# Cross attention with layer norm: 128 instead of 64 rows of weights in each score matmul

## The chip, the core and the metric

The kernel runs on one core of a Trainium2 chip. The time is device microseconds for one execution, and the median over runs is given. The core has a matrix engine (TensorE, PE in the profile; PEld are its weight loads), a vector engine (DVE), a scalar engine (ACT), GpSimd (POOL), a queue engine (SP), and DMA engines that move data beside them. Matmuls write to PSUM, which has eight banks.

## The reference

Four batches, 2048 queries of 512 features each, 77 context rows per batch, 16 heads of 32 features. A mask excludes context rows; the output is normalised over the features with a gain and an offset.

```python
qs = (q @ wq).reshape(Bq, Lq, H, HD).transpose(0, 2, 1, 3)
ks_ = (k @ wk).reshape(Bq, Lk, H, HD).transpose(0, 2, 1, 3)
vs = (v @ wv).reshape(Bq, Lk, H, HD).transpose(0, 2, 1, 3)
scores = jnp.einsum('bhqd,bhkd->bhqk', qs, ks_) / jnp.sqrt(jnp.float32(HD))
scores = jnp.where(mask[:, None, :, :], -jnp.inf, scores)
attn_w = jax.nn.softmax(scores, axis=-1)
attn = jnp.einsum('bhqk,bhkd->bhqd', attn_w, vs)
attn = attn.transpose(0, 2, 1, 3).reshape(Bq, Lq, H * HD)
out = attn @ wo + q
mu = jnp.mean(out, axis=-1, keepdims=True)
var = jnp.mean((out - mu) ** 2, axis=-1, keepdims=True)
return (out - mu) / jnp.sqrt(var + EPS) * gamma + beta
```

## The kernel before

The 8192 rows of x are cut into 64 tiles of 128 rows; a pair of tiles is a block, and four tiles are a group. The order of all work is written out by hand in the string `ORDER`, one letter per step and a number for the tile, block or group; each engine works through its own share of that order, first in, first out for DVE, ACT, POOL and the SP queue. Buffers and PSUM banks are assigned by hand in `SLOTS`.

For each group the steps are: load x transposed (`g`, L260 to L262, on SP), split it into a high and a low part (`i` on ACT, L265; `j` on POOL, L269), project to queries with three products of the parts (`Q`, L275, 12 matmuls of 128x128 weights and 512 streamed columns for each of four column blocks), and copy the queries out of PSUM (`q`, L289, DVE).

For each tile t: the scores (`S`, L391 to L408, PE), the masked maxima out of PSUM (`T`, L416, DVE, 16 heads one by one), the exponentials with their sums (`e`, L431, ACT), reciprocals (`r`, L441, DVE), normalisation (`n`, L446, POOL), and a transposition in blocks of 32 (`t`, L467, DVE). For each block: regrouping of the transposed weights by twelve DMAs (`P`, L478, mostly on SP), the product with the values (`V`, L492, PE, weights of 96x32), copies of its high and low part (`a`, L521, ACT; `b`, L525, DVE). For each tile again: the output projection (`O`, L548, PE, 12 matmuls), the residual (`+`, L557, DVE), the moments (`s`, L568, L569, DVE), the scale (`v`, `k`, POOL and ACT), gain and offset (`f`, L587, L588, POOL), and the store (`w`, L591, SP). The last 16 tiles take a shorter way at the end (L594 to L617), with the residual added by matmuls with an identity (`X`, L537) for the last eight.

The scores of a tile: heads lie four to a 128-partition column block of the queries, 32 partitions each. For head group g (four of them) and head j within it (four), the weights are the queries of that head, 32 partitions by `SR` rows, and the streamed side is the 77 keys. Each j writes to a PSUM bank of its own (four banks a tile), each g to its own 77 columns of it, and each slice of `SR` rows to its own partitions. With `SR = 64` a weight tile has 32 rows and 64 columns of the array, and eight such tiles fit into the array; the inner loops run over the two row slices and then the four heads. Both operands are 32-bit floats, and a matmul of these leaves two weight loads and two multiplies in the trace.

```python
for g in range(NG):
    for r0 in range(0, P, SR):
        for j in range(GH):
            q = slice(HD * j, HD * (j + 1))
            mm = nc.tensor.matmul(
                sc[j][r0 : r0 + SR, g * NK : (g + 1) * NK],
                qs[q, g, rs.start + r0 : rs.start + r0 + SR],
                kct[q, g, t // TPB, keys_of(j)],
```

In the steady middle the order on PE for a block is: scores of one tile, product with the values of an earlier block, scores of the other tile, two query projections (24 matmuls), two output projections (24 matmuls).

Of the kernel before, what the change touches and what calls it, by code (L numbers as in the profile page):

```python
# [37 lines left out]
MASKED = -3.38e38  # L38
EPS = 1.0e-5
WARM = 9  # L40
SR = 64
NPB = 3
KSCALE = 1.0 / HD**0.5
LATE = 48
# [129 lines left out]
def xattn_layernorm(  # L174
# [75 lines left out]
    def keys_of(h):  # L250
        return slice(TAIL_K, NK2) if h % 2 == 0 else slice(0, NK)
# [139 lines left out]
    def scores(t):  # L391
# [3 lines left out]
# [8 lines that stand above are left out]
# [357 lines left out]
```

## Time and profile before

| what | value |
|---|---|
| median of 3 runs | 526.71 us (525.96 to 527.35) |
| span of the profiled execution | 525.7 us |
| instructions in the profile | 20274 |
| score loads and multiplies (L399) | 4096 and 4096 |
| granted TensorE clock | 0.997 |

The profiled execution's own time is known by its span, from its first to its last instruction; the 1.0 us between it and the median lies around the span. PE's busy time adds up records whose ends are modelled and which overlap, so a group's busy time is its union in time, and the mean of one record is longer than its share. A timeline row gives the start, the length of the merged stretch, engine, line, operation and count, and in brackets the idle time before it and what ended it.

### The profile page before, as it was taken

How to read it: one execution, taken by the hardware profiler on the slowest of the kernel's cores; microseconds unless marked ns; L12 is line 12 of the kernel's file. 1: busy time of each engine (PE TensorE's matmuls, PEld its weight loads, DVE VectorE, ACT ScalarE, POOL GpSimd, SP SyncE). 2: the span in 40 equal slices, each digit the busy share in tenths (PEclk: the TensorE clock that was granted, in tenths of full speed). 3: DMA queues.
4: the chain of work that ended last, by engine and by line, in shares of the span. 5: the costliest groups of instructions: out<-in, count | busy, mean ns of one | idle time of the engine just before them, and what ended most of it. 6: DMA issues, size and time to landing. Idle time of an engine off the chain costs nothing.

```text
span 525.7 us, 20274 instructions
## 1 busy us (share of the span) xinstructions
PE 507.2 (96%) x6845; PEld 388.8 (74%) x6845; DVE 476.0 (91%) x2572; ACT 460.4 (88%) x2215; POOL 405.5 (77%) x371
## 2 busy tenths in 40 slices
PE   9999999999989999999999999999999999999994
PEld 6987777778767777777777777767777777767662
DVE  5798988989979989998989989998998999999997
ACT  6699999998989999999999999999999999987400
POOL 2475736889889889969989887988888689869551
PEclk9999999999999999999999999999999999999998
DMA  8948577785797677988887687797868987388555
GB/s 300 401 125 241 148 205 196 195 236 147 205 243 226 189 197 225 217 219 219 215 225 207 178 224 226 184 254 195 213 190 225 259 251 189 91 219 218 158 176 199
DMA packets 59261, 110.85 MB, mean 211 GB/s; under 512 B 9430, under 2 KB 11758, under 8 KB 59158
## 3 DMA queue, kind: packets, MB, share of 16 engines
q1 hardware_dynamic: 55702, 102.75, 69.1%
q0 software_dynamic: 2496, 5.77, 3.9%
q10 hardware_dynamic: 960, 1.05, 0.8%
q8 instruction: 54, 0.88, 0.7%
q14 instruction: 49, 0.40, 0.3%
HBM read 41.79 MB, written 16.78 MB: 111 GB/s over the span
## 4 chain that ended last, share of the span: by engine, by line
PE 51%; DVE 12%; DMA 10%; POOL 9%; SPq 9%; ACT 5%; issue 3%; POOLq 0%; DVEq 0%
PE pq L275 20%; PE po L548 15%; PE sc L399 7%; SPq L478 6%; PE pa L492 6%; DMA PT<-B 6%; ACT pbuf L431 4%; POOL o L587 3%; DVE B L467 3%; POOL o L588 2%; POOL pbuf L446 2%; DVE pbuf L416 2%; PE pv L326 2%; DMA stage_a<-xT 1%; POOL xtl L269 1%
## 5 line engine op out<-in xcount | busy, mean ns | idle before, releaser
L431 ACT ACTIVATE pbuf<-pbuf,nm 128x77 f32<-128x77 f32 x1024 | 352.7, 350 | 16.2 <-DVE nm L416 13.4
L431 ACT ACTIVATION_READ_ACCUMULATOR pbuf<-pbuf,nm 128x1 f32 x1024 | 194.6, 190 | 0.0
L416 DVE CUSTOM_DVE_ANT_0 pbuf<-sc,mb 128x77 f32<-128x77 f32 x1024 | 170.2, 231 | 9.6 <-PE sc L399 8.5
L446 POOL TENSOR_TENSOR pbuf<-pbuf,ri 128x1232 f32<-128x1232 f32 x63 | 142.8, 2267 | 39.4 <-DVE ri L441 23.6
L467 DVE STREAM_TRANSPOSE B<-pbuf 128x1280 f32<-128x1280 f32 x64 | 96.1, 1502 | 9.8 <-POOL pbuf L446 5.4
L548 PE MATMUL po<-woh,AH 128*128 128x512 f32 x256 | 102.6, 401 | 0.0
L548 PE MATMUL po<-woh,AL 128*128 128x512 f32 x256 | 100.1, 391 | 2.3 <-DVE AL L525 2.3
L275 PE MATMUL pq<-xth,wqh 128*128 128x512 f32 (+1 forms) x256 | 101.8, 398 | 0.2
L548 PE MATMUL po<-wol,AH 128*128 128x512 f32 x256 | 99.8, 390 | 0.0
L275 PE MATMUL pq<-xtl,wqh 128*128 128x512 f32 (+1 forms) x256 | 98.3, 384 | 0.0
L275 PE MATMUL pq<-xth,wql 128*128 128x512 f32 (+1 forms) x256 | 98.1, 383 | 0.0
L416 DVE DVE_READ_ACCUMULATOR2_ANT nm<- 128x1 f32 x1024 | 83.9, 82 | 0.0
L399 PEld LDWEIGHTS sc<-kct,q 32*64 32x64 f32 x4096 | 52.8, 130 | 32.9 <-issue 17.1
L587 POOL TENSOR_TENSOR o<-o,gam 128x512 f32<-128x512 f32 x48 | 62.5, 1302 | 13.7 <-ACT o L583 13.4
L269 POOL TENSOR_TENSOR xtl<-xtf,xth 128x1024 fp32r<-128x1024 f32 x28 | 67.3, 2403 | 6.7 <-ACT xth L265 6.6
L399 PE MATMUL sc<-kct,q 32*64 32x77 f32 x4096 | 63.6, 238 | 8.4 <-issue 3.8
L588 POOL TENSOR_TENSOR o<-o,bet 128x512 f32<-128x512 f32 x48 | 62.4, 1300 | 3.8
L492 PE MATMUL pa<-PT,vsb 96*32 96x256 f32 x992 | 59.9, 382 | 0.0
L521 ACT CAST AH<-pa 128x512 fp32r<-128x512 f32 x64 | 36.4, 572 | 25.0 <-DVE st L596 10.6
L548 PEld LDWEIGHTS po<-woh,AL 128*128 128x128 f32 x256 | 48.0, 188 | 13.8 <-DVE AL L525 3.5
L548 PEld LDWEIGHTS po<-woh,AH 128*128 128x128 f32 x256 | 48.0, 188 | 13.7 <-issue 2.0
L275 PEld LDWEIGHTS pq<-xth,wqh 128*128 128x128 f32 x256 | 48.1, 188 | 12.0 <-PE sc L399 0.5
(108 smaller groups left out, 666.0 us busy)
## 6 DMA issues: line engine op xcount, KB each, us to landing
PT<-B SPq DMA_DIRECT2D x343, 128.0 KB
xtf<-xT SPq DMA_DIRECT2D x28, 512.0 KB
o<-x SPq DMA_DIRECT2D x56, 256.0 KB
out<-o SPq DMA_DIRECT2D x56, 256.0 KB
PT<-B POOLq DMA_DIRECT2D x25, 128.0 KB, 3.8
xtf<-xT SPq DMA_DIRECT2D x4, 256.0 KB
stage_a<-wq SPq DMA_DIRECT2D x4, 256.0 KB
stage_a<-wk SPq DMA_DIRECT2D x4, 256.0 KB
```

The source lines that it names most:

```text
L269: nc.gpsimd.tensor_tensor(l[:, c : c + 2], fx.pop((g, c)), xh[g][:, c : c + 2].bitcast(F32), ALU.subtract)
L275: nc.tensor.matmul(pq, w[:, c, m * P : (m + 1) * P], r[g][:, c, rs], start=(n == 0), stop=(n == 11))
L399: mm = nc.tensor.matmul(sc[j][r0 : r0 + SR, g * NK : (g + 1) * NK], qs[q, g, rs.start + r0 : rs.start + r0 + SR], kct[q, g, t // TPB, keys ...
L416: nc.vector.tensor_tensor_reduce(pb[:, h // 2, (h % 2) * NK : (h % 2 + 1) * NK], scs[t][j][:, g * NK : (g + 1) * NK], mb[:, t % TPB, keys_ ...
L431: nc.scalar.activation(pb[:, h // 2, (h % 2) * NK : (h % 2 + 1) * NK], pb[:, h // 2, (h % 2) * NK : (h % 2 + 1) * NK], AF.Exp, bias=nmax[t ...
L446: nc.gpsimd.tensor_tensor(pv, pv, rv.to_broadcast((P, NP, 2, NK)), ALU.mult)
L467: nc.vector.transpose(bt.rearrange("p c q r -> p q c r"), pbuf[t % NPB].rearrange("p q (c r) -> p q c r", c=5),)
L492: nc.tensor.matmul(pas[b, g // 2][HD * j : HD * (j + 1), (g % 2) * BLK : (g % 2 + 1) * BLK], vsb[:, 2 * b // TPB, h % 2, HD * (h // 2) : H ...
L521: nc.scalar.copy(*at_part(once(ahs, b, [P, NG, BLK], F32R, "AH"), b, i, by_tile))
L548: nc.tensor.matmul(pos[t], a[:, c, rs], w[:, c, :], start=(first and c == 0 and n == 0), stop=(c == NC_D - 1 and n == 2),)
L587: nc.gpsimd.tensor_tensor(o, o, gam, ALU.mult)
L588: nc.gpsimd.tensor_tensor(o, o, bet, ALU.add)
```

## The change

One constant is doubled. The loop over row slices in `scores` then has one pass, and every score matmul takes the 128 rows of a tile as weights.

```diff
 EPS = 1.0e-5
 WARM = 9
-SR = 64
+SR = 128
 NPB = 3
 KSCALE = 1.0 / HD**0.5
```

A tile then has 16 score matmuls in the program in place of 32. Each has weights of 32 partitions by 128 columns, streams the same 77 keys, and writes all 128 partitions of its bank's 77 columns. Such a weight tile takes 32 rows and 128 columns of the array, and four of them fit. No other function reads the constant.

## The prediction

> **What bounds the kernel now.** I read the page first, then the busy time by stretches, then one period of the middle as a timeline, then the score matmuls alone.
>
> ```profile
> span 525.7 us, 20274 instructions
> ...
> PE 507.2 (96%) x6845; PEld 388.8 (74%) x6845; DVE 476.0 (91%) x2572; ACT 460.4 (88%) x2215; POOL 405.5 (77%) x371
> ```
>
> ```profile
> 22.00:132.05 110.05, 109.14 (x1556) 85.12 (x1557) 100.77 (x607) 105.22 (x527) 77.94 (x55) 1.00 0.69 194
> 132.05:283.63 151.58, 148.35 (x2081) 114.81 (x2081) 138.94 (x786) 145.07 (x697) 132.18 (x112) 1.00 0.79 213
> 283.63:298.38 14.75, 14.75 (x209) 11.45 (x209) 14.01 (x80) 13.74 (x65) 12.90 (x12) 1.00 0.77 217
> 283.63:406.06 122.43, 119.00 (x1666) 91.99 (x1665) 111.06 (x630) 114.75 (x552) 106.74 (x89) 1.00 0.78 212
> 406.06:479.80 73.74, 72.80 (x1143) 53.63 (x1143) 70.22 (x420) 71.34 (x370) 58.88 (x58) 1.00 0.75 208
> 479.80:525.70 45.90, 37.33 (x280) 25.69 (x276) 42.18 (x101) 11.66 (x48) 22.93 (x41) 0.97 0.58 181
> ```
>
> The columns are the stretch and its length, then the busy time of PE, weight loads, DVE, ACT and POOL, the granted clock, the DMA share and GB/s. From 22 to 480 us, where all score matmuls lie, PE is busy for 449.3 of 457.8 us at the full clock, and in the period 283.63 to 298.38 (two tiles of 128 rows) for all of it. DVE is next with 14.01 of 14.75. After 479.8 DVE leads, but no score matmul runs there. So a microsecond added to PE before 480 is a microsecond on the end, less what PE's few waits swallow:
>
> ```profile
> PE sc L399 <- issue: 3.8, 4, 1.6
> PE po L548 <- DVE AL L525: 2.3, 3, 1.0
> PE sc L399 <- DMA o<-x: 2.0, 2, 1.3
> ...
> PE sc L399 <- DVE q L289: 0.9, 2, 0.7
> PE sc L399 <- DMA PT<-B: 0.6, 1, 0.6
> PE sc L399 <- DVE nm L416: 0.6, 2, 0.4
> ```
>
> These are all of PE's waits at the score matmuls but one of 0.2 us, in total, times and longest: 3.8 + 2.0 + 0.9 + 0.6 + 0.6 = 7.9 us. The 2.3 us of L548 belong to the tail.
>
> Now one period on PE:
>
> ```profile
> 283.63 0.95 PE L399 MATMUL sc<-kct,q 32*64 32x77 f32 x64
> ...
> 284.51 1.93 PE L492 MATMUL pa<-PT,vsb 96*32 96x256 f32 x32
> ...
> 286.38 0.95 PE L399 MATMUL sc<-kct,q 32*64 32x77 f32 x64
> ```
>
> One tile's scores are 64 pairs of a weight load and a multiply (the program has 32 matmuls a tile, and each leaves two pairs in the trace). From their first start to the start of what comes next is 284.51 - 283.63 = **0.88 us**. What sets these 0.88 us is seen by counting how many have started by a given time:
>
> ```profile
> 283.62:283.69 0.07, 0.06 (x8) 0.06 (x9) 1.00 1.12 234
> ...
> 283.62:283.75 0.13, 0.12 (x9) 0.12 (x17) 1.00 0.83 205
> 283.62:283.81 0.19, 0.18 (x16) 0.18 (x24) 1.00 0.83 237
> 283.62:283.88 0.26, 0.25 (x24) 0.25 (x32) 1.00 0.94 268
> 283.62:283.94 0.32, 0.31 (x32) 0.31 (x33) 1.00 0.95 250
> 283.62:284.05 0.43, 0.42 (x37) 0.42 (x37) 1.00 0.83 233
> 283.62:284.15 0.53, 0.52 (x44) 0.52 (x49) 1.00 0.80 236
> ...
> 283.62:284.35 0.73, 0.72 (x63) 0.72 (x64) 1.00 0.85 275
> ```
>
> The counts in brackets are multiplies and loads. The first 32 multiplies come in rounds of eight, one for each of the eight 32x64 tiles: 8, 16, 24, 32, the last three counts 0.065 us apart, and the loads run one round ahead. The second round starts (9th multiply) just before 283.75, about 0.117 after the first. So in this half the multiplies' streaming decides, about 0.067 us a round, and the loads are hidden. The other 31 need 0.41 us, and now loads and multiplies start together (37 and 37): nothing lies ready, so this half is paced by the issue of instructions, about 13 ns a pair. The last multiply has started just after 284.35, and the next work starts some 0.15 us later.
>
> **The change part by part.** It halves the pairs of a tile (64 to 32, so 4096 to 2048 in the run), and makes each one wider: 128 columns of weights go into a 32x128 tile, of which there are four. The streamed side stays at 77 columns. The four tiles do the work of eight in the same eight rounds (32 / 4 = 64 / 8). By streaming alone nothing changes, and the issue gets twice the room. What grows is the weight load.
>
> ```profile
> L399 PEld LDWEIGHTS sc<-kct,q 32*64 32x64 f32 x4096 | 52.8, 130 | 32.9 <-issue 17.1 <-DVE nm L416 8.8 <-DMA PT<-B 3.9
> L275 PEld LDWEIGHTS pq<-xtl,wqh 128*128 128x128 f32 x256 | 48.2, 188 | 8.9 <-POOL xtl L269 0.3 <-issue 0.2
> ```
>
> ```profile
> 23.87 0.19 PEld L275 LDWEIGHTS pq<-xth,wqh 128*128 128x128 f32 x1 [0.26 <-PE sc L399]
> 23.98 0.19 PEld L275 LDWEIGHTS pq<-xtl,wqh 128*128 128x128 f32 x1
> 24.10 0.19 PEld L275 LDWEIGHTS pq<-xth,wql 128*128 128x128 f32 x1
> 24.23 0.19 PEld L275 LDWEIGHTS pq<-xth,wqh 128*128 128x128 f32 x1
> 24.34 0.19 PEld L275 LDWEIGHTS pq<-xtl,wqh 128*128 128x128 f32 x1
> ```
>
> A load of 64 columns lasts 130 ns in the records and one of 128 columns 188: 58 ns for 64 columns. With the array idle, a second load of 128 columns starts 0.11 us after the first (23.87, 23.98). So I price a load at about 0.053 us for 64 columns and 0.107 for 128, behind a fixed latency that is hidden. The counts fit: the second round begins a load and a stream (0.053 + 0.064) after the first, later ones a stream.
>
> The Trainium skill (TensorE: Matmul & The Clock Gate, section "LDWEIGHTS (loading the stationary operand)") says that a 32x128 load takes as long as a 128x128 one, since the columns count and not the rows. No run here shows a 32x128 load; by that rule the sum below would stand as it is.
>
> Today's 0.053 hides under the 0.067 of a round. The new 0.107 doesn't: a tile of the array takes its next weights once the multiply before has begun (the loads are one round ahead, never two), so its period is the load, and the 0.067 of streaming lies under it. I take 0.110 a round (0.11 between the two loads). Low end: 0.107, nothing between loads. High end: 0.120, the spacing of the loads at 24.10, 24.23, 24.34, each beside a multiply.
>
> A tile's scores then: first load 0.107, seven rounds of 0.110 = 0.770, the four tiles' starts 7 ns apart (eight starts in the first 0.06 us) 0.02, and 0.155 from the last start to the next work: 1.052 us in place of 0.88, **+0.17 us**, times 64 tiles **+10.9 us**. With 0.107 it is +0.149 and +9.5; with 0.120 +0.24 and +15.4.
>
> Given back: PE's issue stalls.
>
> ```profile
> q8 instruction: 54, 0.88, 0.7%
> ```
>
> ```profile
> 252.92 0.95 PE L399 MATMUL sc<-kct,q 32*64 32x77 f32 x64
> 253.81 1.93 PE L492 MATMUL pa<-PT,vsb 96*32 96x256 f32 x32
> 255.67 0.80 PE L399 MATMUL sc<-kct,q 32*64 32x77 f32 x46
> 257.38 0.42 PE L399 MATMUL sc<-kct,q 32*64 32x77 f32 x18 [0.90 <-issue]
> ```
>
> Fetched instructions came in 54 packets, 16 KB each. The 6845 pairs are 13,690 instructions, so these look like PE's own, some 250 a packet. In the stall at 257.38 the scores stand still inside a tile, with no engine behind it: since 252.92 PE had used up 128 + 64 + 92 instructions. After the change this whole stretch has 64 + 64 + 64, less than a packet, so such stalls should mostly go: of 3.8 us I take 2.2 back (bounds 0 and 3.8). Of the 4.1 us of waits for DMA and DVE, a slower PE swallows some, since whoever is late gains 0.34 us a period: 1.5 (bounds 0 and 4.1). DVE's maxima (L416) start 0.17 us later in each tile, covered by PE's own lateness: ACT, POOL and the DMAs behind them have the same work in a longer period. Banks, semaphores and the order of the program stay; no DMA is added, none moved.
>
> Sum: 525.7 + 10.9 - 2.2 - 1.5 = 532.9 us of span. The median of the runs is 526.71, 1.0 above this execution's span, so **533.9 us**, 1.4% slower. Own range: 526.7 + 9.5 - 7.9 = 528.3 to 526.7 + 15.4 = 542.1.
>
> **The rivals.**
>
> *Faster: wide loads are as quick as two narrow ones.* Today the two 64-column tiles over the same 32 rows must both be filled within a round, 2 x 0.053 in 0.067, so they load side by side. If one 128-column load uses both ways, it takes 0.053 and hides, and eight rounds of streaming remain, all out of the queue: 0.053 + 7 x 0.067 + 0.02 + 0.155 = 0.70, -0.18 a tile, -11.7 in all, with 2.2 of stalls -13.9. DVE's 14.01 in a period of 14.75 leaves room, but waits for DVE and DMA would grow; I count two thirds, -9.3: 517.4. Against it: 128-column loads follow each other at 0.11 even where nothing else runs. It decides as soon as a load stays under 0.067. Chance 0.13.
>
> *No change: the first load is hidden.* If the first wide load of a tile is put under the tail of the work before, a tile costs 0.945, +0.065, times 64 +4.2, less 3.7: 527.2. Against it: loads of the scores stand 0.35 us idle before each tile.
>
> ```profile
> 283.63 0.79 PEld L399 LDWEIGHTS sc<-kct,q 32*64 32x64 f32 x64 [0.35 <-issue]
> ```
>
> Chance 0.08.
>
> *Far slower: a load waits for its own tile's multiply.* The period is then 0.107 + 0.067 = 0.174, a tile 0.107 + 7 x 0.174 + 0.175 = 1.50, +0.62, times 64 +39.7; with all 6.3 us of DMA and DVE waits and fetch stalls swallowed (2.2 + 4.1) it ends at 560. Against it: rounds of 0.067 with loads of 0.053 in them, and projections that follow each other at 0.12 with a load of 0.107 beside each. That the four tiles run one after another, so that the change doesn't do what it says, would be 32 x 0.107 + 0.175 = 3.6 us a tile, +2.7, times 64 +174: 700; today's eight run at once, and I count it in here. Chance of both 0.05.
>
> The Trainium skill (TensorE: Matmul & The Clock Gate, section "The mechanism" of the packing part) states this rule: a load overlaps running matmuls only where the row group differs. Here each row group always has its own multiply running, so by it the result would be this rival's 560; the rows just named speak against it.
>
> **How the numbers follow.** Forecast 0.74, rivals 0.13, 0.08 and 0.05. A difference of 0.3% (1.6 us) is about what these runs can tell from none. Faster takes the first rival and a little of the second, 0.14; same takes most of the second and the forecast's lowest corner, 0.10; slower is 0.76. The range runs from 526 to 543: it holds the forecast's own and the second rival, and leaves out 0.18.
>
> **What would show it.** The scores' multiplies should be 2048, 32 a tile, in rounds of four about 0.11 us apart, with a load at the start of each round and its multiply after it; first start to next start about 1.05 us; loads of about 188 ns; a period near 15.1 us with PE full; fewer "issue" stalls inside tiles. Rounds at 0.067 show the first rival, at 0.17 the third. If tiles take 1.05 us and the end still doesn't move, the step from PE's time to the end was wrong; if the issue stalls stay, that of the fetch.

## The result and the profile after

| | kernel before | kernel after |
|---|---|---|
| median, 20 runs each | 526.48 us (523.44 to 531.38) | 529.10 us (527.63 to 531.17) |
| ratio | 1 | 1.0042, 95% interval 1.0023 to 1.0061 |
| profiled execution: span | 525.7 us | 526.0 us |

The kernel became 2.6 us slower where 7.2 us were forecast: sign and range held, the size did not. The profiled execution of the new kernel took 527.80 us for its span of 526.0, so 1.8 us lie around the span, and not the 1.0 that the prediction had from the median. The profiled execution of before, with the same 1.8, was one of about 527.5, 1.1 above its median; the one of after lies 1.3 below its own. That is why the spans differ by 0.3 us and the medians by 2.6.

The page of the kernel after, its head, the fetch queue and the chain of waits:

```profile
span 526.0 us, 16084 instructions
...
PE 514.5 (98%) x4797; PEld 398.4 (76%) x4797; DVE 477.8 (91%) x2572; ACT 460.7 (88%) x2215; POOL 404.7 (77%) x371
...
q8 instruction: 38, 0.62, 0.6%
...
PE 81%; DVE 12%; POOL 3%; DMA 1%; issue 1%; SPq 1%; POOLq 0%; DVEq 0%
```

The last line has this counterpart in the page of before:

```profile
PE 51%; DVE 12%; DMA 10%; POOL 9%; SPq 9%; ACT 5%; issue 3%; POOLq 0%; DVEq 0%
```

PE's own work went from 51% to 81% of the chain: it now runs through with hardly a wait. DMA, SP's queue, POOL and ACT, which together held 33% of it, hold 5%. PE's waits in the kernel after, all that the view lists, in total, times and longest:

```profile
PE sc L399 <- DVE q L289: 2.1, 2, 1.5
PE po L548 <- DVE AL L525: 1.9, 2, 1.0
PE pw L628 <- DVE ident L620: 1.2, 1, 1.2
```

The issue stalls (3.8 us before) and the waits for DMAs at the scores (2.0 and 0.6) are gone. The groups of score loads and multiplies, after, and the multiplies of before:

```profile
L399 PEld LDWEIGHTS sc<-kct,q 32*128 32x128 f32 x2048 | 62.9, 186 | 25.1 <-issue 10.7
L399 PE MATMUL sc<-kct,q 32*128 32x77 f32 x2048 | 72.2, 277 | 2.1 <-DVE q L289 2.1
```

```profile
L399 PE MATMUL sc<-kct,q 32*64 32x77 f32 x4096 | 63.6, 238 | 8.4 <-issue 3.8 <-DMA o<-x 2.0 <-DVE q L289 0.9
```

One block after, and the same by counts of multiplies and loads in the first tile (columns as in the prediction, without ACT and POOL):

```profile
284.43 1.13 PE L399 MATMUL sc<-kct,q 32*128 32x77 f32 x32
285.50 1.93 PE L492 MATMUL pa<-PT,vsb 96*32 96x256 f32 x32
287.36 1.13 PE L399 MATMUL sc<-kct,q 32*128 32x77 f32 x32
```

```profile
284.43:284.50 0.07, 0.07 (x4) 0.07 (x4) 0.00 (x0) 1.00 0.00 0
284.43:284.60 0.17, 0.17 (x4) 0.17 (x8) 0.00 (x0) 1.00 0.08 12
284.43:284.71 0.28, 0.28 (x8) 0.28 (x12) 0.00 (x0) 1.00 0.05 7
284.43:284.82 0.39, 0.39 (x12) 0.39 (x16) 0.00 (x0) 1.00 0.07 11
```

A tile takes 1.07 us from start to start by the rows (1.061 by the trace's finer stamps, in every steady tile), against 0.88 before. The multiplies come in rounds of four, one round in each 0.11 us, with the loads one round ahead. Then the middle as a whole:

```profile
100.00:400.00 300.00, 300.00 (x2844) 234.74 (x2843) 274.94 (x1555) 285.87 (x1368) 263.82 (x225) 1.00 0.76 212
283.00:298.11 15.11, 15.11 (x146) 11.84 (x145) 14.32 (x80) 13.72 (x59) 12.90 (x12) 1.00 0.72 212
```

In 300 us of the middle PE is never idle. A block takes 15.11 us: of the 16 from 164 to 405 us, 15 take just this and one takes 15.17. Before, the quickest block took 14.72, and the same 16 blocks, from 163 to 406 us, took 15.18 in the mean. So in these two executions the new kernel is slower than an undisturbed block of before and yet as quick in the mean, because it has no disturbed ones.

Where that went is seen in the trace of before, PE's timeline at its score tiles; the brackets are the idle time in front and its releaser:

```profile
148.42 1.02 PE L399 MATMUL sc<-kct,q 32*64 32x77 f32 x64 [1.58 <-issue]
```

```profile
165.97 1.34 PE L399 MATMUL sc<-kct,q 32*64 32x77 f32 x64
167.25 0.50 PE L275 MATMUL pq<-xth,wqh 128*128 128x512 f32 x1
```

```profile
348.82 0.37 PE L399 MATMUL sc<-kct,q 32*64 32x77 f32 x10 [1.05 <-issue]
349.12 0.50 PE L275 MATMUL pq<-xth,wqh 128*128 128x512 f32 x1
```

```profile
392.66 0.90 PE L399 MATMUL sc<-kct,q 32*64 32x77 f32 x59
393.83 0.35 PE L399 MATMUL sc<-kct,q 32*64 32x77 f32 x5 [0.27 <-issue]
394.11 0.50 PE L275 MATMUL pq<-xth,wqh 128*128 128x512 f32 x1
```

```profile
406.06 0.94 PE L399 MATMUL sc<-kct,q 32*64 32x77 f32 x64 [0.76 <-DMA o<-x]
```

There are two kinds. **Inside a tile** (349, 394, and 257 in the prediction; 166 is a slight one): PE stands with no engine behind it, and then goes on at the slow pace of issue. These four tiles took 1.28, 2.06, 2.21 and 1.45 us from start to start in place of 0.88, together 3.5 us, of which only 0.90 + 1.05 + 0.27 = 2.2 show as idle. **Ahead of a tile**, between an output projection and the first score matmul of a block, which also waits for the DMAs of the values' product behind it: 1.58, 0.64, 1.27 and 0.76 us at 148, 223, 314 and 406, 4.25 in all. The first bears "issue", but it stands at such a boundary, with a wait on semaphores in front of it.

If each PE instruction is given the time to the start of the next one, the two profiled spans are balanced like this: scores +6.4 (the pace adds 64 x 0.18 = 11.5, inner stalls and waits give 5.1 back), the last projection before a score tile -5.0 (the waits ahead of tiles), the rest -1.1; in all +0.3.

### The profile page after: what moved, and what is told of

Read it like the earlier page. It is cut to its first block, busy times and chain, and to the rows that moved or that the text cites. A ratio compares the mean times of both kernels' runs of the same rounds, so it can differ in the third digit from the quotient of the medians.

```text
span 526.0 us, 16084 instructions
## 1 busy us (share of the span) xinstructions
PE 514.5 (98%) x4797; PEld 398.4 (76%) x4797; DVE 477.8 (91%) x2572; ACT 460.7 (88%) x2215; POOL 404.7 (77%) x371
## 3 DMA queue, kind: packets, MB, share of 16 engines
q10 hardware_dynamic: 960, 1.05, 0.7%
## 4 chain that ended last, share of the span: by engine, by line
PE 81%; DVE 12%; POOL 3%; DMA 1%; issue 1%; SPq 1%; POOLq 0%; DVEq 0%
PE pq L275 30%; PE po L548 26%; PE sc L399 12%; PE pa L492 9%; DVE B L467 2%; DVE pbuf L416 2%; DMA PT<-B 1%; POOL pbuf L446 1%; PE pk L298 1%; PE pq L655 1%; DVE o L617 1%; PE pv L326 1%; DVE AL L525 1%; DVE q L289 1%; DVE st L596 1%
## 5 line engine op out<-in xcount | busy, mean ns | idle before, releaser
L416 DVE DVE_READ_ACCUMULATOR2_ANT nm<- 128x1 f32 x1024 | 85.2, 83 | 0.0
L399 PEld LDWEIGHTS sc<-kct,q 32*128 32x128 f32 x2048 | 62.9, 186 | 25.1 <-issue 10.7
L399 PE MATMUL sc<-kct,q 32*128 32x77 f32 x2048 | 72.2, 277 | 2.1 <-DVE q L289 2.1
```

Source lines behind the costliest of these rows:

```text
L399: mm = nc.tensor.matmul(sc[j][r0 : r0 + SR, g * NK : (g + 1) * NK], qs[q, g, rs.start + r0 : rs.start + r0 + SR], kct[q, g, t // TPB, keys ...
L416: nc.vector.tensor_tensor_reduce(pb[:, h // 2, (h % 2) * NK : (h % 2 + 1) * NK], scs[t][j][:, g * NK : (g + 1) * NK], mb[:, t % TPB, keys_ ...
```

## The experiments

Times are medians; ratios are to the kernel before, run beside them on the same chip (its medians there: 526.2 and 526.4, 530.1 for the kernels with a cut values' product and for the last one, 526.0 for the two of changed order). Two theories share the question why 11.5 us of PE's work cost 2.6. "Slack": PE was hardly the bound before, each block now has room, and waits of every kind fall into it. "Instructions": half as many score instructions end the stalls inside tiles, and only the waits for data go by slack.

### PE's work added without fewer instructions, and PE's work added once more

Six score matmuls of a tile are done twice with 64 rows (the last head group, heads 0 to 2), which adds to PE what the change adds; four are done twice with 128 rows.

```diff
+        for r0 in range(0, P, SR):
+            for j in range(3):        # GH with 128 rows
+                q = slice(HD * j, HD * (j + 1))
+                nc.tensor.matmul(
+                    sc[j][r0 : r0 + SR, (NG - 1) * NK : NG * NK],
...
```

> 64 rows as before, and in each tile six score matmuls of the last head group are done a second time (the same values to the same place): 12 more pairs of load and multiply, priced at 13 to 17 ns of issue each, so PE's work for a tile goes from 0.88 to about 1.06 us, as with 128 rows, but the instructions rise by 1536 in place of falling by 4096. Theory 'slack' (before, PE had waits in hand because others arrive at about 15.1 us a period, so a longer PE just fills them): 528 to 532, as with 128 rows, and PE's waits at the scores fall from 8.4 us to under 4. Rival 'instructions' (the time came back because PE had half as many score instructions to fetch and issue): nothing comes back, 526.5 + 64 x 0.18 = 538, range 535 to 540, with the issue waits at 3.8 us or more.

Measured 536.29 us, ratio 1.0201 (1.0164 to 1.0237). PE's waits with the 64 rows and the six extra matmuls:

```profile
PE sc L399 <- issue: 3.8, 6, 1.7
...
PE pq L275 <- POOL rn L584: 1.3, 1, 1.3
...
PE sc L399 <- DMA PT<-B: 1.0, 1, 1.0
PE sc L412 <- issue: 0.6, 1, 0.6
PE sc L399 <- DMA out<-o: 0.3, 1, 0.3
```

An undisturbed block takes 15.12 us, as in the changed kernel, yet the time is 7.2 us above that kernel's 529.1. The waits ahead of tiles fell from 4.25 to 1.3 us: there slack works. The stalls inside tiles grew from 2.2 us to 3.8 + 0.6, and the 1.3 put down to POOL stands at the same place in the instruction stream as they do (below). So slack alone is refuted: with PE's work for a block the same as in the changed kernel, more instructions kept the stalls inside tiles and enlarged them. How much of the 8.9 us (11.5 - 2.6) each theory has is not settled by this run.

> 128 rows, and the four matmuls of the last head group are done a second time: 8 more pairs, two more rounds of 0.112 us, +0.22 us a tile. Theory 'slack': the waits are used up, so all of it shows: 529.1 + 64 x 0.22 = 543.4, range 541 to 545. Rival 'another engine sets the period': the time moves less than half of that, under 536.

Measured 541.16 us, ratio 1.0288 (1.0265 to 1.0312): 12.1 above the changed kernel for 64 x 0.223 = 14.3 us of PE's work. With no waits left to swallow it, added work on PE reaches the end nearly in full. PE's path was the bound, and the prediction's conversion of work to time was sound, as long as nothing is given back.

### What the stalls inside tiles are

The windows between the ends of the four stalls, before (busy time of PE, loads, DVE, ACT, POOL, each with its count):

```profile
166.82:257.38 90.56, 89.02 (x1257) 68.82 (x1256) 84.01 (x474) 87.45 (x419) 79.03 (x66) 1.00 0.79 211
257.38:348.82 91.44, 89.03 (x1256) 69.01 (x1256) 83.35 (x472) 86.77 (x416) 80.00 (x69) 1.00 0.79 217
348.82:393.83 45.01, 44.74 (x630) 34.47 (x630) 41.02 (x237) 42.46 (x203) 38.46 (x32) 1.00 0.74 203
```

1257 and 1256, 1256 and 1256, then half of it, 630 and 630. With PE's register and semaphore instructions, which the views don't count, the trace has 2560, 2560 and 1280 between them: 10, 10 and 5 times 256. A packet of q8 holds about as many: 54 packets for 13,960 PE instructions before, 38 for 9,770 after. The place where one packet is used up and the next begins is called its border below. In the kernel with the six extra matmuls the first three are 2 x 256 apart each:

```profile
151.09:169.49 18.40, 15.66 (x252) 12.21 (x252) 14.95 (x80) 15.97 (x79) 14.52 (x16) 1.00 0.88 238
169.49:185.24 15.75, 15.53 (x255) 12.11 (x255) 13.29 (x79) 13.19 (x64) 12.14 (x9) 1.00 0.63 168
```

All these stalls of that kernel, the one put down to POOL too, lie at instruction 193 or 194 modulo 256, counted from the trace's first PE instruction, and so do the four of the kernel before. By the stamps, PE used up the 256 instructions before each of the four stalls of the kernel before in 3.2 us, and the next came 3.5 to 4.5 us after the border before. So the densest stretch of the program (scores, values' product, scores) uses instructions up about as fast as they are brought, or faster. The time of a packet varies: two packets of 3.1 us, at 211 and 302 us, passed without a stall, and one stall each came after a packet of 6.0 us (with the six extra matmuls) and of 7.2 us (in the kernel with half of its tiles changed, below). What sets the time that a packet takes to come was not tried. After the change, from 100 us to the tail, no 256 instructions are used up in under 9.8 us.

So far this is a matter of place. The next pair takes the dense stretch away: in 19 blocks the second tile's scores go behind the first query product, and the copy of that product on DVE goes ahead of the tile's maxima. For one of the blocks, in the order's words:

```diff
-S30 +22 n28 w21 P13.5s V12 ... S31 x26 s22 ... T30.3 Q34 ... T31.0 ... q34
+S30 +22 n28 w21 P13.5s V12 ... x26 s22 ... T30.3 ... Q34 S31 q34 T31.0 ...
```

> 64 rows as before, same instructions; in the 19 blocks from tile 16 on whose order on PE is scores, values, scores, queries, queries, the second tile's scores are put behind the first query product (12 matmuls, 2.7 us), and the copy of that product on DVE ahead of the second tile's maxima. The densest 256 instructions on PE then take over 5 us in place of 3.2. Theory 'fetch' (PE uses up a packet of 256 instructions faster than the next one comes): the issue stalls inside the score tiles go (3.8 us before, with what follows them some 5), and the time falls by 2 to 5 us unless the later scores bring waits of their own at DVE: ratio 0.990 to 0.997, and PE's wait 'scores on issue' under 0.5 us. Rival 'form' (the stalls belong to score matmuls of 64 rows, wherever they stand): the issue stalls stay at 2 to 5 us, ratio 0.998 or more.

> The same change of order with 128 rows. There are no issue stalls to lose. Theory 'fetch': as the changed kernel, block period 15.11 us, ratio to before 1.002 to 1.007; so the gap between 64 and 128 rows opens to 5 to 9 us, nearer to the 11.5 us that PE's work grew by. Rival 'order' (the new order helps or hurts by itself, through DVE's or ACT's queues): this kernel moves by as much as the one with 64 rows, and the gap stays at 2 to 3 us.

Measured 536.76 us with 64 rows, ratio 1.0219 (1.0183 to 1.0256), and 542.80 with 128, ratio 1.0329 (1.0300 to 1.0358). Both are slower than forecast, by a cost of the order itself: an undisturbed block takes 14.97 us with 64 rows (14.72 before) and 15.29 with 128 (15.11), and there is one long wait at 190 us. PE's waits at the scores and projections with 64 rows:

```profile
PE po L548 <- DVE nm L416: 3.9, 1, 3.9
...
PE sc L399 <- DVE nm L416: 1.7, 3, 1.3
...
PE sc L399 <- DMA PT<-B: 0.9, 1, 0.9
...
PE sc L399 <- issue: 0.2, 1, 0.2
```

The issue stalls went from 3.8 us to 0.2, with the same 64 rows and the same instructions, and the 0.2 lies ahead of a tile and not at a packet's border. In the reordered stretch no packet is used up in under 5.8 us. This is the forecast of the theory "fetch", and the rival "form" is refuted; the times of the forecast missed.

The gap between 64 and 128 rows opened as well, from 2.6 to 6.0 us (542.80 - 536.76). The 3.4 between are close to the 3.5 that the four stalled tiles cost before, but they can't be put down to the stalls alone, since two other things changed with the order. Of the 4.25 us of waits ahead of tiles, 0.85 and the 0.2 are left with 64 rows too. And the block with the long wait does not cost the same in both kernels: it takes 7.0 us more than an undisturbed one with 64 rows and 5.8 with 128, for 3.9 us of waiting. PE and its granted clock (third number from the end) there, with 64 rows:

```profile
190.25 0.77 PE L548 MATMUL po<-woh,AH 128*128 128x512 f32 x1 [3.90 <-DVE nm L416]
```

```profile
191.00:195.00 4.00, 4.00 (x11) 3.12 (x10) 0.00 (x0) 2.70 (x9) 0.00 (x0) 0.50 0.79 235
```

Behind the wait the granted clock was 0.50, and output projections came 0.43 us apart in place of 0.23; with 128 rows fewer of them did.

Another pair cuts the matmuls of the values' product by their columns, into two and into four, in the changed kernel.

```diff
+                for c in range(4):      # range(2), columns by c, in the other
+                    c0 = (g % 2) * BLK + c * 64
                     nc.tensor.matmul(
-                        pas[...][..., (g % 2) * BLK : (g % 2 + 1) * BLK],
+                        pas[...][..., c0 : c0 + 64],
...
-                        pt[:NK2, :, h % 2, h // 2].rearrange("p i t r -> p t i r"),
+                        pt[:NK2, 2 * (c % 2) : 2 * (c % 2) + 2, h % 2, h // 2, c // 2],
```

> 128 rows in the scores as in the changed kernel; each matmul of the values' product is cut into two of 128 columns. The array streams the same columns, but the stretch scores, values, scores now has 64 + 128 + 64 = 256 instructions, as many as it had with 64 rows, in about 4.1 us in place of 3.6. Theory 'fetch' (a packet of 16 KB is 256 instructions, and the next is there 3.5 to 4.4 us after the last was begun): issue stalls come back at packet borders, small ones, 0 to 0.9 us each, 0 to 6 us in all, time 529 to 536. Rival 'form' (the stalls of before belonged to the score matmuls of 64 rows as such, not to the number of instructions in a stretch): no issue stalls over 0.1 us, time 528 to 531.

> 128 rows in the scores as in the changed kernel; each matmul of the values' product is cut into four of 64 columns: 64 + 256 + 64 = 384 instructions in scores, values, scores, 128 pairs in the product's 1.93 us (15 ns a pair). Theory 'fetch': about a quarter of the packet borders have the whole packet before them inside this stretch, used up in 1.9 to 2.9 us, and PE then stands 0.6 to 2.4 us with no engine behind it; some 16 such stalls, 15 to 35 us, time 543 to 565; all of them 256 instructions apart or a multiple of it. Rival 'form': no such stalls; the product may take up to 0.3 us longer a block by the issue of its pairs, 528 to 540.

The cut in two took 532.13 us, ratio 1.0069 (1.0028 to 1.0111), with one wait of 0.3 us on issue ahead of a tile and none at a border. It decides nothing: the quickest 256 instructions take 3.9 us there, and no border fell on them (5.0 us at the quickest). The cut in four took 605.07 us, ratio 1.1452 (1.1384 to 1.1519), far over both forecasts, because the product itself grew to 4.4 us:

```profile
253.25 4.43 PE L494 MATMUL pa<-PT,vsb 96*32 96x64 f32 x128
257.62 0.67 PE L399 MATMUL sc<-kct,q 32*128 32x77 f32 x12
259.65 0.89 PE L399 MATMUL sc<-kct,q 32*128 32x77 f32 x20 [1.36 <-issue]
```

128 pairs in 4.37 us are 34 ns a pair, so a packet lasts 4.1 us or more there, and the sixteen stalls of the forecast, worked out for packets of 1.9 to 2.9 us, could not come. What the last row shows is still worth its place: a tile with 128 rows, standing 1.36 us inside itself at instruction 194 of a packet. So the stall doesn't belong to the 64-row form.

Two earlier attempts, four no-operation instructions on PE behind each score matmul, and the same number among the projections, were to raise the count alone.

```diff
+                    for _ in range(4):
+                        nc.tensor.nop(nofuse=True, hint="pad")
```

> 128 rows, and four empty PE instructions behind each of a tile's 16 score matmuls: PE has as many instructions in scores, values product, scores as before (128 + 64 + 128), and the array has the same work as with 128 rows. Theory 'fetch' (before lost time because PE used up 256 instructions in about 3.2 us, quicker than the next 16 KB arrive; 128 rows ended that): stalls inside the scores come back, each at the same place modulo 256 instructions, and the time rises from 529.1 to 530.5 to 535. Theory 'slack' (arrivals by DMA and other engines, filled up by a longer PE): no change, 528.5 to 530. If an empty instruction takes longer to issue than a pair (over 17 ns), the scores get longer by that alone, which the rounds of four would show.

> 128 rows, and the same 4096 empty PE instructions, but among the query and output projections, where a pair takes 0.227 us. Theory 'fetch': the number of instructions as such costs nothing, only their rate in the scores: 528.5 to 530, no stalls at the 16 KB borders. Rival 'number of instructions' (the transfers of 16 KB more get in the way of others): as before's stalls, 531 or more.

Behind the scores: 750.45 us, ratio 1.424 (1.418 to 1.430). Among the projections: 539.21 us, ratio 1.0237 (1.0205 to 1.0269). The no-ops follow each other 71 ns apart in the trace, so they paced PE by themselves; behind the scores the granted clock also fell to 0.865 in the mean. A tile there:

```profile
416.09 4.14 PE L399 MATMUL sc<-kct,q 32*128 32x77 f32 x32
```

In neither kernel are 256 instructions used up in under 6.4 us, and neither stalled at a border. Both missed their forecasts by the no-operations' own time, and they don't tell the theories apart. The second shows only that as many packets as before (54) pass without a stall at that pace.

### The waits ahead of a tile

The first score matmul of a block carries the waits of the values' product behind it. Without them (the waits then stand at the product), with 64 and with 128 rows:

```diff
-                    if first:
-                        early_waits(mm, t)
```

> 64 rows, without the rule that a tile's first score matmul already waits for the regrouping transfers that only the following values product reads (that product still waits for them itself). Theory 'slack': PE runs ahead and waits for these arrivals, so the waits move from the scores to the values product and shrink by at most 0.88 us each; some 1 to 3 us less than before, 523.5 to 526. Rival 'instructions': these waits aren't what PE loses, no change, 526.5.

> 128 rows, without the rule that the scores wait for the regrouping transfers of the values product behind them. With 128 rows PE doesn't wait for these any more: no change, 528 to 530. If typical runs, unlike the profiled one, still wait there, 526 to 528.

With 64 rows 525.89 us, ratio 0.9996 (0.9969 to 1.0024); with 128 rows 530.56, ratio 1.0075 (1.0045 to 1.0104). PE's waits at the product, and on issue, in the first:

```profile
PE pa L490 <- DMA PT<-B: 0.6, 2, 0.3
PE sc L399 <- issue: 0.6, 3, 0.2
PE pa L490 <- PE sc L399: 0.4, 2, 0.2
PE pa L490 <- DMA out<-o: 0.4, 2, 0.2
```

In this execution the waits ahead of tiles are gone and small ones stand at the product, and its span is 521.2 us; but by the time it took (523.0 with the 1.8 around it) it is the quickest end of that kernel's runs (522.99 to 529.35), and its median is that of the kernel before. Where its slower runs lose the gain isn't in the trace. The row of issue is worth a look: its three waits, at 299, 344 and 390 us, lie at borders, at instruction 193 or 194 again. This kernel has the same dense stretch as the kernel before, and six of its borders fall on it, each after a packet used up in 3.25 to 3.4 us. Three passed without a stall, and at the other three the tiles took only 0.5 us longer each, 1.4 in all. So what the stalls cost is no constant of the program: 3.5 us is the cost in one execution of the kernel before. With 128 rows no such wait was left to move, and nothing was won.

Half of each: even tiles with 128 rows, odd ones with 64.

```diff
+        sr = SR if t % 2 else 2 * SR
```

> Even tiles with 128 rows, odd tiles with 64: PE's work for a pair of tiles rises by 0.18 in place of 0.36 us, to about 14.9 a period. Theory 'slack': still inside the waits, 525 to 528, no more than 1.5 above before. A PE that sets the end alone: 526.5 + 32 x 0.18 = 532.

Measured 528.12 us, ratio 1.0030 (1.0003 to 1.0056), so some 1.6 us for half of PE's extra work (32 x 0.18 = 5.8), at the upper end of what "slack" foretold. An undisturbed block takes 14.93 us; one border stall (0.7 us) and one wait ahead of a tile (0.7) are left. So half of the room was enough for most of the waits ahead of tiles to go, in this execution.

### Less work on PE

The score operands are rounded to the one-pass 32-bit format (fp32r), so that a matmul has one load and one multiply: the low part of queries and keys is left out of the scores. Each matmul streams 78 columns.

```diff
-    kct = const.tile([P, NG, NB, NK2], F32, name="kct")
+    kct = const.tile([P, NG, NB, NK2], F32R, name="kct")
...
-                        sc[j][r0 : r0 + SR, g * NK : (g + 1) * NK],
+                        sc[j][r0 : r0 + SR, g * 78 : (g + 1) * 78],
```

> 128 rows, and the score operands rounded for a single pass: one pair of load and multiply for each matmul in place of two (16 pairs a tile, four rounds), 78 columns streamed. This leaves out the low part of the scores' operands. A tile falls from 1.06 to about 0.61 us, PE's work for a period from 15.11 to 14.21, and its instructions fall again. Theory 'slack': DVE has 14.01 and ACT 13.74 us of work in a period and arrivals come at 14.7 to 15, so only part of the 28.6 us shows: 512 to 522. If PE alone set the end, 500.5.

> Score operands rounded to fp32r (one pass, the low parts left out) with 128 rows, and the wait of the first score matmul for the values' DMAs taken out. Theory 'arrivals' (with the scores' PE work halved, PE stands at the scores for data of the values' product that it could take later): 1 to 5 us less than with that wait, 511 to 515. Rival 'other engines' (DVE's and ACT's own work sets the 14.6 us period now): no change, 515.5 to 517.

Measured 516.37 us, ratio 0.9823 (0.9781 to 0.9865); without the early waits 515.77, ratio 0.9767 (0.9704 to 0.9830): the intervals overlap, and no gain of the waits can be told. A tile, and the middle, of the first:

```profile
290.88 0.64 PE L399 MATMUL sc<-kct,q 32*128 32x78 f32 x16
291.45 1.93 PE L492 MATMUL pa<-PT,vsb 96*32 96x256 f32 x32
```

```profile
100.00:400.00 300.00, 293.71 (x2304) 222.47 (x2303) 280.83 (x1608) 293.13 (x1411) 271.42 (x231) 1.00 0.80 217
```

A tile takes 0.57 us, 0.49 less than in the changed kernel, 31 us in all, and 12.7 of these arrive. PE has 14.2 us of work a block, but blocks come 14.66 apart in the mean (16 blocks from 159 to 394 us): ACT is busy for 293 of 300 us. An estimate of the scale for the kernel before follows from it: if 14.66 is the pace that the other engines hold by themselves, its 14.72 us of PE work a block stand only 0.06 above it, and a late transfer soon reaches PE. The changed kernel's 15.11 stand 0.45 above. No run took these other engines' work away to test it. Both versions are quicker than either kernel of the change, at the price of the scores' low parts.

## Why the prediction was right in sign and wrong in size

- **The cost of a wide load: right.** 1.061 us a tile for a predicted 1.052, rounds of 0.112 us for 0.110, loads of 186 ns for 188, 64 x 0.18 = 11.5 us for 10.9. The Trainium skill (TensorE: Matmul & The Clock Gate, section "LDWEIGHTS (loading the stationary operand)") has a 32x128 load take as long as a 128x128 one; the trace agrees, 186 ns and 188.
- **The first rival, wide loads as quick as two narrow ones: wrong.** Rounds of 0.067 us would have been seen. **The second, the first load hidden: wrong in its mechanism.** It foretold 527.2 us, which is nearer than the forecast, but by tiles of 0.945 us, and each takes 1.061.
- **A load that waits for its tile's multiply: wrong.** 0.112 us a round, not 0.174; by the order of the program each load starts some 0.045 us after its own tile's multiply, whose record lasts 0.27, and so beside it. By the Trainium skill (same page, section "The mechanism") loads overlap multiplies only where the row group differs; the trace contradicts that here.
- **From PE's time to the end: right where nothing waits.** The 14.3 us of the repeated 128-row matmuls came out as 12.1.
- **Given back: the step that failed.** The prediction had "of 3.8 us I take 2.2 back" and, of DMA and DVE waits, "1.5 (bounds 0 and 4.1)", 3.7 in all. By the medians 11.5 - 2.6 = 8.9 us came back (11.2 between the two traced executions, which lie on opposite sides of their medians). Three things were wrong in it. First, a stall was priced by its idle time. The four border stalls showed 2.2 us idle but cost 3.5 in the traced execution, since the tile goes on at the issue's pace. Second, the 3.8 us taken for stalls of the fetch held the longest "issue" wait, 1.58 us at 148.42, which stands at a block's boundary; the 2.2 taken back equal the idle time of the other three, but the prediction has no count that leads to them. Third, the waits for data were thought of as sharing 0.34 us a block with PE. All 4.25 us ahead of tiles went, and two at DVE's maxima (some 1.3 us in the tile at 116) with them, for one new wait of 1.5 us in the tile at 42 us. The 64-row kernel with the same PE work kept 1.3 us of those ahead of tiles, which suggests that room alone takes most of them; its own stalls gave it some more room (15.53 us a block in the mean).
- **The fetch as a mechanism: right.** Packets went from 54 to 38, a stretch of scores, product and scores now holds less than one, and no stall is left at a border.
- **Outside the span:** 1.8 us, not 1.0. The execution that the sum was made against lay about 1 us above its kernel's median, and the 1.0 had taken that out, so nothing of the miss comes from it.

What stays open: how much each run of the kernel before loses, and how the 8.9 us divide between stalls and waits in a typical run. Its runs spread over 8 us and the new ones over 3.5, which fits waits that come and go, but only one execution was traced.

## What to carry to other kernels

Price a stall by how much later the next work starts, from start to start against an undisturbed repetition, not by the idle time in front of an instruction; and compare the quickest block with the mean block, because the difference is what a slower but smoother engine may get back. When idle time has no engine behind it, count the instructions between such places: equal counts point to the fetch, and then fewer instructions, or the same ones less densely placed, are worth more than a shorter busy time.

## What the runs showed of the hardware that was not expected

- PE's instructions came in packets of 256. Where the kernel before used one up in 3.2 us, it stood still four times, until 3.5 to 4.5 us had passed since the border before; 5.2 and 5.3 us occurred once each in the kernel with the six extra matmuls. It didn't always stand: two packets of 3.1 us passed in the kernel before, and three of 3.3 us in the one without early waits.
- After PE had stood idle for 3.9 us in the reordered kernel, the granted clock was 0.50 over the next 4 us and 128x512 multiplies came 0.43 us apart in place of 0.23. The stalls and waits of up to 1.6 us in the kernel before left it at 1.00.
- Cutting the matmuls of the values' product (96x32 weights) from 256 streamed columns to 128 left its time almost as it was, 1.86 and 1.95 us; cutting them to 64 raised it to 4.37, 34 ns a pair where those of 128 columns take 31. Which part of a pair sets this, the load or something else, was not tried.
- PE no-operations came 71 ns apart, also at a granted clock of 0.999; that is about five times the 13 ns of a load and multiply pair of the scores.
